# Layer 0's first hidden spectrum taken from modes that are at hand, instead of from a forward transform of q

## The chip, the cores and the metric

The kernel runs on one core of one Trainium2 chip. The metric is the device time of one execution in microseconds (us). Engines: TensorE (PE) multiplies matrices; VectorE (DVE), ScalarE (ACT) and GpSimd (POOL) work elementwise; SyncE (SP) issues the transfers.

## The reference

Two layers follow one another; only the first (L0) is touched. Its input is four batches of T=32 images of 128x128 pixels.

```python
xn = _inorm(xa, norm1_w, norm1_b)          # per image
k, q, v = fno(xn, K..), fno(xn, Q..), fno(xn, V..)   # 32 heads, spectral + skip
p_attn = softmax(scores over the 32 images of a batch)
p = fno(einsum(p_attn, v), Pcw, Psw)
a = _inorm(p + xa, attn_w, attn_b)
an = _inorm(a, norm2_w, norm2_b)
m = gelu(_inorm(spectral(an, m0cw)) + skip(an))
m = _inorm(spectral(m, m1cw)) + skip(m)
x = x + _inorm(m, mon_w, mon_b) + a
```

A spectral convolution keeps 64 x 33 modes of an image's two-dimensional real Fourier transform, multiplies them by a table, and transforms back. p + xa is linear in the modes of x: a mix over the batch's images, and the image's own part.

## The kernel before, in words

A batch of layer 0 has 128 (w) x 32 (images) x 128 (c) values, w on the partitions. The tile framework schedules the work from the program's order and its waits; `behind(a, b)` only keeps a behind b. Buffers belong to tags with a fixed number of them. Instructions of one engine run in order, and DMAs are issued by SP in order. A batch goes through these stages:

1. Front, for the next batch (`image_rows`, `image_moments`, `spectra_of_images`, L388 to L604): ACT squares of x (xx, L395), sums over images by TensorE (rows, L401), the group norm, the modes of x (pz, it, em, std), scaled by n_s (the inverse deviation times norm1_w) into xe, xm, xx, and written to HBM as xd (L559).
2. Attention weights (L653): products pa, pb, scores, softmax; the weights ph leave for HBM and come back as pr. `skip_matrix` (L780) makes bd, the image mix of the skip part: cm on TensorE, cd, cp and bd on DVE.
3. Mix (loop at L961): for five ranges of modes and four quarters of images SP broadcasts xd to xb (four buffers, L969), ACT copies it to PSUM (xw), POOL and DVE multiply by the weights (u, L989, L993), TensorE sums over images (po, L926). Between these, the skip part is turned (pxt) and applied (sk) into q, and the next batch's x is loaded.
4. py (L1027) brings the mixed modes to images, yf (L225, L227 inside `evacuate`, which divides copies over ACT and DVE) is their copy; the inverse (pv L319, four L324) gives p's images, added to q (L1042); bn_stats (L1044) and `stats` give the moments m.
5. `spectra(0, q)`: the forward transform of q (pz L305, px L1123, part, spec), its squares weighed to the variance v0 of the spectral part (L1149 on); the next batch's image rows; `row_products` (y, L342) and `four_images` (L356, L358) give the spectral part's image; the 32 additions of q into x (L1079).
6. GELU: g (L1212), its activation (L1216), bn_stats (L1224), then `spectra(1)` of g, the second variance, and the result added to x.

DVE's bn_stats, additions and copies and ACT's copies share stages 4 to 6. `roots` keeps single instructions for `behind`. Layer 1 lists its work by hand (`tc.manual_schedule`); its first pieces run inside the last batch.

## Time and profile before

| | us |
|---|---|
| runs: median (range) | 2872.17 (2871.64 to 2875.78) |
| profiled execution, of which the span | 2870.23, 2868.6 |
| PE, DVE, ACT, POOL busy in the span | 2720.7, 2175.5, 2315.7, 2035.3 |
| py's start in batches 0 to 3, from the span's start | 131.55, 323.60, 515.70, 707.76 |
| batch 0: m, first g, n_s of the next batch | 160.31, 185.69, 222.06 |
| first d of layer 1 | 833.07 |

Busy times are sums of instructions, which overlap between engines; a long busy time is no bound by itself. A line of the timeline gives start, length, engine, line of the source, operation, output<-inputs, shape and count; in brackets what the engine waited for.

### The profile page before, as it was taken

What the parts mean: (1) busy time and instruction counts of PE and PEld (TensorE: products, weight loads), DVE (VectorE), ACT (ScalarE), POOL (GpSimd) and SP (SyncE); (2) the same over time, 40 slices, a digit from 0 to 9 for tenths busy, and PEclk for the clock granted to TensorE, in tenths of its full rate; (3) what the DMA queues carried; (4) which work ended last, traced back from release to release, by engine and by line L of the source; (5) the groups of instructions that cost most, each with busy time, mean ns of one, the idle gap of its engine ahead of it and who ended that gap; (6) DMA issues with size and microseconds to landing.
All of it is one profiled execution on the core that took longest, in us unless ns stands there. A gap on an engine that the chain in (4) does not pass through costs nothing.

```text
span 2868.6 us, 52910 instructions
## 1 busy us (share of the span) xinstructions
PE 2720.7 (95%) x19638; PEld 1379.6 (48%) x19638; DVE 2175.5 (76%) x4830; ACT 2315.7 (81%) x3243; POOL 2035.3 (71%) x1804
## 2 busy tenths in 40 slices
PE   8898999988879999999999999999999999999996
PEld 5565664654644444445444444544444454444442
DVE  5888788778766677777787776778788677877777
ACT  3555466465459999999999999999999999999990
POOL 2706418137028998998998988898898888878872
PEclk9999999999989999999999999999999999999998
DMA  4403204114030101002101000110100010010000
GB/s 103 125 1 106 88 8 149 39 42 138 3 81 23 41 1 41 8 14 47 40 2 34 16 16 19 41 27 23 41 1 16 20 34 19 16 34 1 16 12 19
DMA packets 151153, 107.72 MB, mean 38 GB/s; under 512 B 36302, under 2 KB 140017, under 8 KB 150897
## 3 DMA queue, kind: packets, MB, share of 16 engines
q1 hardware_dynamic: 147633, 102.26, 13.5%
q8 instruction: 155, 2.54, 0.4%
q10 hardware_dynamic: 3264, 2.10, 0.3%
q14 instruction: 101, 0.83, 0.1%
HBM read 63.86 MB, written 19.50 MB: 29 GB/s over the span
## 4 chain that ended last, share of the span: by engine, by line
PE 60%; ACT 7%; DVE 5%; POOL 3%; issue 2%; DMA 0%; SPq 0%; DVEq 0%; POOLq 0%; ACTq 0%
PE d L1869 26%; PE po L1888 15%; PE px L1770 6%; PE n L1869 5%; ACT r L1938 3%; DVE r L1943 1%; ACT e L1954 1%; DVE xc L1779 1%; ACT r L1950 1%; PE pl L1739 1%; POOL e L1946 1%; PE pz L1571 1%; PE pa L1701 1%; PE pt L1533 1%; PE pz L1586 1%
## 5 line engine op out<-in xcount | busy, mean ns | idle before, releaser
L1943 DVE TENSOR_TENSOR r<-n,r 128x1024 f32<-128x1024 f32 (+1 forms) x1056 | 961.9, 953 | 457.3 <-PE n L1869 327.9
L1938 ACT ACTIVATE r<-d 128x1024 f32<-128x1024 f32 (+1 forms) x1056 | 793.6, 803 | 63.6 <-PE n L1869 51.4
L1946 POOL TENSOR_TENSOR e<-r 128x512 f32<-128x512 f32 x528 | 673.4, 1275 | 213.0 <-DVE r L1943 211.4
L1950 ACT ACTIVATE r<-r 128x1536 f32<-128x1536 f32 x528 | 783.6, 1484 | 16.8
L1947 POOL TENSOR_TENSOR e<-e,r 128x512 f32<-128x512 f32 x528 | 671.8, 1272 | 41.4
L1869 PE MATMUL d<-qe,ke 32*128 32x512 f32 (+3 forms) x2304 | 604.5, 601 | 16.9 <-ACT r L1938 12.8
L1869 PE MATMUL n<-qe,ke 32*128 32x512 f32 (+3 forms) x2304 | 604.6, 601 | 0.0
L1888 PE MATMUL po<-e,kx 128*128 128x512 f32 (+3 forms) x1152 | 594.4, 605 | 3.0 <-POOL e L1959 3.0
L1869 PE MATMUL n<-qf,kf 32*128 32x512 f32 (+3 forms) x2304 | 550.8, 553 | 0.0
L1869 PE MATMUL d<-qf,kf 32*128 32x512 f32 (+3 forms) x2304 | 549.1, 552 | 0.0
L1779 DVE SCALAR_TENSOR_TENSOR xc<-px,wgt,xc 128x128 f32<-128x128 f32 x1024 | 354.5, 349 | 34.9 <-PE px L1770 5.2
L1888 PEld LDWEIGHTS po<-e,kx 128*128 128x128 f32 x1152 | 175.4, 188 | 376.1 <-issue 297.6
L1954 ACT ACTIVATE e<-e 128x512 f32<-128x512 f32 x528 | 324.2, 614 | 14.7 <-POOL e L1947 14.7
L1869 PEld LDWEIGHTS d<-qe,ke 32*128 32x128 f32 x2304 | 176.5, 183 | 302.0 <-ACT r L1938 273.2
L1869 PEld LDWEIGHTS d<-qf,kf 32*128 32x128 f32 x2304 | 219.1, 185 | 164.4 <-issue 152.6
L1770 PE MATMUL px<-we,x2t 128*128 128x512 f32 (+3 forms) x644 | 271.0, 515 | 5.7 <-DVE xc L1779 2.0
L989 POOL TENSOR_TENSOR u<-xb,gb 128x858 f32<-128x858 f32 (+1 forms) x112 | 220.6, 2008 | 42.4 <-PE po L926 37.6
L1869 PEld LDWEIGHTS n<-qf,kf 32*128 32x128 f32 x2304 | 227.5, 185 | 24.8 <-issue 17.2
L1140 POOL TENSOR_TENSOR spec<-part,part 128x512 f32<-128x512 f32 x16 | 25.7, 1609 | 284.8 <-DVE gn_r_t L253 93.0
L993 DVE TENSOR_TENSOR u<-xw,gb 128x858 f32<-128x858 f32 (+1 forms) x208 | 215.6, 1105 | 6.7 <-ACT xw L980 3.1
L1770 PEld LDWEIGHTS px<-we,x2t 128*128 128x128 f32 x644 | 119.3, 193 | 140.4 <-issue 116.8
L1869 PEld LDWEIGHTS n<-qe,ke 32*128 32x128 f32 x2304 | 176.8, 183 | 10.9 <-DVE r L1943 1.5
(425 smaller groups left out, 3409.3 us busy)
## 6 DMA issues: line engine op xcount, KB each, us to landing
xb<-xd SPq DMA_DIRECT2D x128, 214.5 KB
xc<-x SPq DMA_DIRECT2D x29, 512.0 KB
x<-x SPq DMA_DIRECT2D x16, 512.0 KB
qf<-qe SPq DMA_DIRECT2D x64, 128.0 KB
out<-xc SPq DMA_DIRECT2D x15, 512.0 KB
x<-in_x SPq DMA_DIRECT2D x14, 512.0 KB
xb<-xd SPq DMA_DIRECT2D x32, 198.0 KB
kf<-ke SPq DMA_DIRECT2D x32, 128.0 KB
```

The source lines that it names most:

```text
L989: weighed = nc.gpsimd.tensor_tensor(u, xb, gk, ALU.mult)
L993: weighed_last = nc.vector.tensor_tensor(u, xw, gk, ALU.mult)
L1770: nc.tensor.matmul(px[:, at_e : at_e + m], x2t[:, k * P : (k + 1) * P], we[:, own[0] : own[0] + m], start=True, stop=True,)
L1779: nc.vector.scalar_tensor_tensor(xc[:, k], px[:, i], wgt[:, k, e : e + 1], xc[:, k], ALU.mult, ALU.add)
L1869: nc.tensor.matmul(o, k, q, start=turn == 0 or g > 0, stop=turn == 1 or g > 0)
L1888: nc.tensor.matmul(sums[c, h][:, q0 : q0 + c1 - c0], kx[:, jb], e[:, c0:c1], start=jb == 0, stop=is_last and q0 > 2 * P, skip_group_check= ...
L1938: nc.scalar.activation(r[:, g], d, AF.Ln, scale=1.0 / DSCALE)
L1943: nc.vector.tensor_tensor(r[:, g], part, r[:, g], ALU.mult)
L1946: nc.gpsimd.tensor_tensor(e, r[:, 1], r[:, 2], ALU.add)
L1947: nc.gpsimd.tensor_tensor(e, e, r[:, 0], ALU.add)
L1950: nc.scalar.activation(r, r, AF.Exp, scale=-1.0)
L1954: nc.scalar.activation(e, e, AF.Exp)
```

## The change

q's modes are no longer taken from q. They are the mixed modes (py) plus the modes of the batch's images, mixed by the skip matrix. For that xd keeps x's modes times the inverse deviation alone (plain), and norm1_w goes into the value weights (v_raw, hv). Eight DMAs a batch read xd back as xs, which holds images on the partitions. `first_product` adds xs times by_part onto py in PSUM, two DVE products with the first layer's table and a POOL addition make modes_of_q; `to_columns` and `inverse_of` make the image of the spectral part from it. v0 comes from the squares of modes_of_q. The transform of q, its row products and its flat part are gone. `skip_matrix` computes cm by small matmuls and spreads it with one more matmul, and stands behind the second half's row products. Image rows go to four column groups of TensorE instead of two. `unfold`, `edge_row` and the tables carry the scalings along; 133 constant columns and four small table loads are added. Additions into x are divided: 8 ahead of GELU, 8 inside it, 16 behind it.

```diff
...
+    def image_squares(xt, earlier=None):
+        parts = []
         for g in GROUPS:
             xx2 = grp.tile([P, GI, C], F32, name="xx2", tag="pr", bufs=6)
             square = nc.scalar.activation(xx2, xt[:, g : g + GI], AF.Square)
-            if "q_r" in roots:
-                behind(square, roots["q_r"])
+            if earlier is not None:
+                behind(square, earlier)
+            parts.append(xx2)
+        return parts
...
+        rows8 = ps.tile([P, 4, C], F32, name="rows8", tag="b")
+        for g, xx2 in zip(GROUPS, parts):
             for h in range(2):
                 m = g // 4 + h
                 for k, src in enumerate((xt[:, 4 * m : 4 * m + 4], xx2[:, 4 * h : 4 * h + 4])):
+                    r = 64 * k + 32 * (m % 2)
                     mm = nc.tensor.matmul(
-                        rows8[32 * k : 32 * k + 32],
+                        rows8[r : r + 32],
                         one_of_8[:, 7 - m : 39 - m],
                         src,
-                        start=m == 0,
-                        stop=m == 7,
+                        start=m < 2,
+                        stop=m > 5,
                     )
                     products.append(mm)
-        ev = grp.tile([64, 4, C], F32, name="ev", tag="pr", bufs=6)
-        nc.scalar.copy(ev, rows8)
+        ev = grp.tile([P, 4, C], F32, name="ev", tag="pr", bufs=6)
+        copied = nc.scalar.copy(ev, rows8)
+        if earlier is not None:
+            behind(copied, earlier)
...
-                nc.tensor.matmul(s12[k][:, j::4], ev[r, j], ident[r, r], start=True, stop=True)
+                r = slice(64 * k, 64 * k + 64)
+                nc.tensor.matmul(s12[k][:, j::4], ev[r, j], one_row[r], start=True, stop=True)
...
+            plain = grp.tile([P, half, KY], F32, name="plain", tag="fold")
+            nc.vector.tensor_tensor(
+                plain.rearrange("p (k i) y -> p i k y", i=2),
+                std[:, :, :, :KY],
+                yr[:, t].rearrange("p (k i) -> p i k", i=2).unsqueeze(3).to_broadcast([P, 2, pairs, KY]),
+                ALU.mult,
+            )
+            to_rows(xd, t, plain)
...
+            u32 = small.tile([m, T], F32, name="u32", tag="u32")
+            nc.vector.scalar_tensor_tensor(u32, o32, twice_low[:m], yr[:m], ALU.mult, ALU.mult)
...
+            for c0, rev in ((v_raw[:, :, 0, ri], v_rev), (pw[:, :, 0, ri], p_rev)):
+                behind(nc.vector.tensor_tensor(c0, c0, rev[:, :, ri], op), normed[4])
+                nc.vector.tensor_scalar(c0, c0, 0.5, None, ALU.mult)
...
+        root = scalars(ALU.mult, "root", ve, yr)
+        root = scalars(ALU.mult, "roots", same, root)
+        own_root = one("own_root")
+        nc.vector.tensor_reduce(own_root, root, AX.X, ALU.add)
         sel = scalars(ALU.mult, "sel", same, ysc)
+        own = one("own")
+        nc.vector.tensor_reduce(own, sel, AX.X, ALU.add)
+        by_four = small.tile([P, 2, 4, 4], F32, name="by_four", tag="cp")
         for h in range(2):
             r = slice(32 * h, 32 * h + 32)
-            cm = ps.tile([P, T, 16], F32, name="cm", tag="a")
-            mm = nc.tensor.matmul(cm, pv[r].to_broadcast([NH, P]), ph[r], start=True, stop=True)
-            if earlier is not None:
-                behind(mm, earlier)
-            cd = grp.tile([P, T, 16], F32, name="cd", tag="v", bufs=3)
-            nc.vector.tensor_tensor(cd, cm, sel.unsqueeze(2).to_broadcast([P, T, 16]), ALU.mult)
-            nc.vector.tensor_reduce(
-                cp[:, 16 * h : 16 * h + 16], cd.rearrange("p s t -> p t s"), AX.X, ALU.add
+            cm = ps.tile([P, 4], F32, name="cm", tag="a")
+            for t in range(16):
+                j = 32 * (t % 4)
+                mm = nc.tensor.matmul(
+                    cm[j : j + 32, t // 4 : t // 4 + 1], ph[r, :, t], pv[r], start=True, stop=True
+                )
+                if earlier is not None:
+                    behind(mm, earlier)
+            nc.vector.tensor_tensor(
+                by_four[:, h],
+                block.unsqueeze(1).to_broadcast([P, 4, 4]),
+                cm.unsqueeze(2).to_broadcast([P, 4, 4]),
+                ALU.mult,
             )
-        nc.vector.tensor_add(cp, cp, same)
+        cp = ps.tile([P, 2, T], F32, name="cp", tag="a")
+        nc.tensor.matmul(cp[:, 0], alike, by_four.rearrange("p h k j -> p (h k j)"), start=True, stop=True)
+        nc.vector.scalar_tensor_tensor(cp[:, 1], cp[:, 0], own, same, ALU.mult, ALU.add)
         bd = small.tile([P, 4, T], F32, name="bd", tag="bd")
         nc.vector.tensor_tensor(
             bd,
             block.unsqueeze(2).to_broadcast([P, 4, T]),
-            cp.unsqueeze(1).to_broadcast([P, 4, T]),
+            cp[:, 1].unsqueeze(1).to_broadcast([P, 4, T]),
             ALU.mult,
         )
-        return bd
+        by_part = small.tile([P, 2, T], F32, name="by_part", tag="by_part")
+        nc.vector.tensor_tensor(
+            by_part,
+            turn_of.unsqueeze(2).to_broadcast([P, 2, T]),
+            cp[:, 1].unsqueeze(1).to_broadcast([P, 2, T]),
+            ALU.mult,
+        )
+        nc.vector.tensor_scalar(by_part, by_part, own_root, None, ALU.mult)
+        return bd, by_part
...
+    for v in (v_raw.rearrange("p x y r -> p (x y r)"), hv[:, 2:3]):
+        behind(nc.vector.tensor_scalar(v, v, par[:, N1W : N1W + 1], None, ALU.mult), normed[4])
...
+        xy = big.tile([P, 2, KX * KY], F32, name=f"xy_{b}", tag="y")
+        xs = xy[:, 0].rearrange("p (x y) -> p x y", y=KY)
+        yf = xy[:, 1].rearrange("p (t r y) -> p t r y", r=2, y=KY)
+        by_images = [
+            (xs[64 * part + 32 * r : 64 * part + 32 * r + 32, to], front[2][:, r, of])
+            for part in range(2)
+            for r in range(2)
+            for to, of in ((slice(0, KX // 2 + 1), slice(KX // 2, KX + 1)), (slice(KX // 2 + 1, KX), slice(1, KX // 2)))
+        ]
...
+                if x0 and by_images:
+                    to, of = by_images.pop(0)
+                    nc.sync.dma_start(out=to, in_=of)
...
+        modes_of_q = big.tile([P, T, 2, KY], F32, name=f"modes_{b}", tag="spec")
+        pys = {}
+        def rows_of(y0):
             n = min(8, KY - y0)
-            py = ps.tile([P, 8, 2, T], F32, name="py", tag="b")
+            py = ps.tile([P, 8, 2, T], F32, name="py", tag="ba"[y0 // 8 % 2])
+            pys[y0] = py[:, :n]
             for k in range(n):
                 for part in range(2):
                     nc.tensor.matmul(
                         py[64 * part : 64 * part + 64, k],
                         rs[:, :, y0 + k],
                         comb[:, 32 * part : 32 * part + 64],
-                        start=True,
-                        stop=True,
+                        start=k == 0,
+                        stop=k == n - 1,
+                        skip_group_check=True,
                     )
-            evacuate(yf[:, :, :, y0 : y0 + n].rearrange("p t r y -> p y r t"), py[:, :n])
-        if b == 0:
-            mode_tables(weighed_last)
+            copied = nc.scalar.copy(yf[:, :, :, y0 : y0 + n].rearrange("p t r y -> p y r t"), pys[y0])
+            if y0 == GI:
+                roots["rows_copied"] = copied
+        def first_product(y0):
+            py = pys[y0]
+            n = py.shape[1]
+            for k in range(n):
+                for part in range(2):
+                    r = slice(64 * part, 64 * part + 64)
+                    nc.tensor.matmul(
+                        py[r, k], xs[r, :, y0 + k], by_part[r], start=False, stop=k == n - 1, skip_group_check=True
+                    )
+            shape = [P, n, 2, T]
+            table = first_table[:, y0 : y0 + n]
+            one_, two = (
+                grp.tile([P, 8, 2, T], F32, name=f"part{i}", tag="v", bufs=3)[:, :n] for i in (1, 2)
+            )
+            nc.vector.tensor_tensor(one_, py, table[:, :, :1].unsqueeze(3).to_broadcast(shape), ALU.mult)
+            nc.vector.tensor_tensor(
+                two, py[:, :, ::-1], table[:, :, 1:].unsqueeze(3).to_broadcast(shape), ALU.mult
+            )
+            nc.gpsimd.tensor_tensor(
+                modes_of_q[:, :, :, y0 : y0 + n].rearrange("p t r y -> p y r t"), one_, two, ALU.add
+            )
+        starts = range(0, KY, 8)
+        for y0 in starts:
+            rows_of(y0)
+            if y0:
+                first_product(y0 - 8)
+        first_product(starts[-1])
...
+            next_squares = image_squares(loaded, roots["rows_copied"])
+        squares = big.tile([P, T, 2 * KY], F32, name=f"squares_{b}", tag="rs")
+        nc.scalar.activation(squares, modes_of_q.rearrange("p t r y -> p t (r y)"), AF.Square)
+        by_t, y0 = per_image("by_t"), per_image("y0")
+        nc.vector.tensor_reduce(by_t, squares, AX.X, ALU.add)
+        nc.vector.tensor_tensor(y0, squares[:, :, 0], squares[:, :, KY], ALU.add)
+        nc.vector.scalar_tensor_tensor(by_t, y0, half_zero, by_t, ALU.mult, ALU.add)
+        energy_of = sums("ms", ones, by_t, "b")
+        v0 = per_image("v0")
+        nc.vector.tensor_copy(v0, energy_of)
+        qm, qv = stats("q", st, "b")
...
-        spec, sq = spectra(0, q)
-        ahead = []
-        if b + 1 < B:
-            ev, ahead = image_rows(loaded)
-        v0 = weighed("v0", sq, squares, layers[0][2], "a")
-        if ahead:
-            behind(summing["ms"], ahead[-3])
...
+        def to_columns(k):
+            pv2 = ps.tile([2 * KY, 4, P], F32, name="pv2", tag="a")
             for j in range(4):
-                t = image(a, g, j)
+                nc.tensor.matmul(
+                    pv2[:, j],
+                    modes_of_q[:, 4 * k + j].rearrange("p r y -> p (r y)"),
+                    inv,
+                    start=True,
+                    stop=True,
+                )
+            v = grp.tile([2 * KY, 4, P], F32, name="v", tag="v", bufs=3)
+            copied = nc.scalar.copy(v, pv2)
+            if acts:
+                in_order(copied)
+            columns_of_q[k] = v
+        def inverse_of(k):
+            v = columns_of_q[k]
+            if k % 2 == 0:
+                wide[k // 2] = ps.tile([P, 2, 4, C], F32, name="fours", tag="wide")
+            fours[k] = wide[k // 2][:, k % 2]
+            for j in range(4):
+                mm = nc.tensor.matmul(fours[k][:, j], v[:, j], icol, start=True, stop=True)
+            return mm
...
+        def early_rows(k):
+            h, k = divmod(4 * k, GI)
             if k == 0:
                 early.append(grp.tile([P, GI, P], F32, name="z1", tag="z"))
-            in_order(four_rows([gl[:, 8 * h + t] for t in range(GI)], early[h], k, nc.scalar.copy))
-        in_order(four_rows([gl[:, 8 + t] for t in range(GI)], early[1], 4, nc.scalar.copy))
+            in_order(four_rows([gl[:, 8 * h + k + t] for t in range(4)], early[h], k, nc.scalar.copy, 0))
+        early = []
+        columns_of_q = {}
+        for k in range(4):
+            to_columns(k)
+            inverse_of(k)
+        to_columns(4)
+        if b + 1 < B:
+            ev, _ = image_rows(loaded, next_squares)
+            sv = image_moments(ev)
+        to_columns(5)
+        to_columns(6)
+        add_attention(0)
+        gelu(0)
+        gelu(1)
+        inverse_of(4)
+        inverse_of(5)
+        to_columns(7)
+        gelu(2)
+        gelu(3)
+        add_attention(GI, roots["gelu"])
+        inverse_of(6)
+        inverted = inverse_of(7)
+        for k in range(4, 8):
+            gelu(k)
+            early_rows(k - 4)
         if b + 1 < B:
             summed = group_moments(sv, inverted)
-        for g in GROUPS:
-            add_attention(g)
+        for g in GROUPS[2:]:
+            add_attention(g, roots["gelu"])
...
+                if a:
+                    begun = [row_products(spec, a)]
+                    rows_last = roots["rows"]
+                inverted = back(spec, a, last, begun, nc.scalar.copy)
             else:
                 back(spec, a, last_scaled, apart=True)
-            if a == 0 and b + 1 < B:
-                bd = skip_matrix(weights[2], front[4], inverted)
+            if a and b + 1 < B:
+                bd, by_part = skip_matrix(weights[2], front, rows_last)
...
```

## Prediction, made before the changed kernel ran

> **What bounds the kernel now.** I read the slices of the page first, then the waits and timelines of layer 0 by stage. Each digit is a slice of 71.7 us.
>
> ```profile
> span 2868.6 us, 52910 instructions
> ...
> PE   8898999988879999999999999999999999999996
> ...
> DVE  5888788778766677777787776778788677877777
> ```
>
> From slice 13 on (833 us) TensorE never falls below 9: that is layer 1, whose instructions, compared on each engine, have the same order before and after the change. So whatever layer 0 gains or loses reaches the end one for one. Layer 0 is four batches of 192 us (q's first step py starts at 131.55, 323.60, 515.70 and 707.76). Busy times by stage of batch 0 (window; then PE, weight load, VectorE (DVE), ScalarE (ACT), GpSimd (POOL)):
>
> ```profile
> core 0: us, PE busy (x) PEld busy (x) DVE busy (x) ACT busy (x) POOL busy (x), PEclk, DMA share, GB/s
> 131.55:160.31 28.76, 27.43 (x306) 25.79 (x306) 19.24 (x78) 7.69 (x11) 0.00 (x0) 1.00 0.01 2
> 160.31:185.69 25.38, 24.45 (x249) 14.37 (x248) 21.95 (x86) 11.80 (x24) 3.45 (x2) 1.00 0.01 1
> 185.69:203.95 18.26, 14.33 (x129) 8.98 (x128) 16.25 (x71) 16.49 (x41) 0.00 (x0) 1.00 0.01 1
> 203.95:222.06 18.11, 17.75 (x183) 14.73 (x180) 15.95 (x55) 8.73 (x27) 3.02 (x2) 1.00 0.00 1
> 222.06:265.55 43.49, 37.22 (x416) 21.61 (x415) 31.55 (x78) 26.61 (x70) 24.77 (x15) 0.96 0.38 86
> 265.55:323.60 58.05, 52.57 (x641) 25.72 (x640) 54.03 (x53) 35.84 (x82) 51.02 (x26) 1.00 0.56 174
> ```
>
> Rows: (1) py and the inverse of q, up to the moments m; (2) q's forward transform and image rows, up to the first g; (3) GELU; (4) second transform, up to the next batch's n_s; (5) attention; (6) mix. In (2) TensorE is full and DVE fills its waits with additions into x; in (3) and (4) DVE is nearly full: from its timeline, only 1.4 + 1.8 = 3.2 us of waits there; the rest of the unfilled busy sum is issue gaps. So cutting TensorE pays in (2), not in (3) and (4).
>
> **What the Trainium skill says.** "TensorEngine Tiling (Array Packing)", Key Properties: different tiles load weights and multiply in parallel; Instruction Overhead: a matmul costs at least some 60 columns. The trace agrees with the first: the 64x64 products em pass 32 records in 0.82 us (26 ns each), py 132 in 8.03 us (61 ns). "SBUF — State Buffer", Who interferes with whom: a DVE operation with two SBUF inputs is blocked by a GpSimd operation that reads SBUF. The trace agrees: additions into x (two SBUF inputs, 128x128) take 0.35 us, but one took 1.35 at 176.54, inside POOL's spec addition of 175.57 to 177.75, and bd below took 1.97 inside POOL's two u products of 258.78 to 262.77. "DMA: Bandwidth & Descriptors", Issuing engines are not separate DMA queues: all transfers share 16 engines, so new loads meet the mix's broadcasts.
>
> **The change, part by part** (batch 0).
>
> ```profile
> 131.55 8.03 PE L1027 MATMUL py<-cst,rs 128*64 128x64 f32 x132 [0.61 <-ACT rs L1013]
> 140.68 1.96 PE L319 MATMUL pv<-cst,yf 128*66 128x128 f32 x16 [1.09 <-ACT yf L225]
> 142.55 2.05 PE L324 MATMUL four<-icol,v 66*128 66x128 f32 x16
> ```
>
> *First product.* Added: 66 matmuls xs by by_part. At 26 ns 1.7 us, at 61 ns 4.0; they wait between rows of py for ACT's yf copies (1.14 each, all five now on ACT, four squares of 1.05 among them): I add 5.3 (3.4 to 8.0), so the last ends at 131.55 + 8.0 + 5.3 = 144.9. Behind it two DVE products of 0.69 and POOL's strided add, which the trace lacks; the nearest, L1140, takes 1.27 to 2.18. The inverse's v takes its buffer from the y0=24 parts: first v copy at 144.9 + 1.4 + 1.6 = 147.9, first four 148.6 instead of 142.55, 6 us late. The inverse itself stays 13.3 to 14 us (16 groups of about 1 us on PE), m moves from 160.31 to 166.1: **+5.8**.
>
> *q's transform goes.* From m to the first g took 25.4 us. Gone on PE: pz 8.9, px about half of the 13.8 below, y, four, d0, and image rows pass from 0.43 us a pair in two column groups to some 4.1 us in four (po's 0.107 us per record of 429 columns, scaled). v0 now comes from squares of the modes (ACT, 2112 columns, 2.05 by 1.05 per 1024; DVE reduce 2.35), ready while DVE works on the inverse. Left from m to g: the roots' chain of small operations as before, without the waits for ms, and 8 of the 32 additions into x (8 x 0.285 = 2.3), about 10.4 us (9 to 14). New columns and images from the modes (8 groups of 0.97 and 8 of 1.03) run ahead of g on a PE that would idle. g at 176.5 instead of 185.69: **-9.2**.
>
> ```profile
> L1079 DVE SCALAR_TENSOR_TENSOR x<-q,ra,x 128x128 f32<-128x128 f32 x32 | 11.9, 398 | 0.0
> L1123 PE MATMUL px<-z,cst 128*32 128x128 f32 (+1 forms) x192 | 13.8, 314 | 0.0
> L305 PE MATMUL pz<-cst,q 128*128 128x128 f32 x64 | 8.9, 285 | 0.7 <-ACT z L225 0.7
> ```
>
> *Additions into x.* Their 0.0 of idle and their place (165 to 184) show that they filled waits. In the changed order 8 stand inside GELU and 16 behind the last g, ahead of pk: 24 x 0.285 = 6.84 us on a DVE that is full. Also +0.7 for sv, tot and a root; less the 3.2 of waits they can fill, plus 1 for new ones: +5.3. n_s: -9.2 + 5.3 = **-3.9**.
>
> *plain.* Two DVE products a batch (0.72 each, like xx) and u32, less 0.9 of wait at em: pa -3.3. xd's four DMAs per half wait for plain, on SP's queue with the first xb behind them; that has 20 us of cover until the mix.
>
> *Skip matrix.*
>
> ```profile
> 257.28 0.69 DVE L791 TENSOR_TENSOR cd<-cm,sel 128x512 f32<-128x512 f32 x1 [0.43 <-PE cm L787]
> ...
> 260.94 1.97 DVE L797 TENSOR_TENSOR bd<-cst,cp 128x128 f32<-128x128 f32 x1
> ```
>
> DVE loses 2 x (0.69 + 1.02) for about eight small ones (0.2 to 0.4); PE changes four 512-column products for 64 one-column ones (26 to 61 ns, 1.7 to 3.9 us) that now stand behind the last row products, where DVE waits anyway. bd stays exposed to POOL, and by_part has the same shape of operands at half the size. -0.8 (0 to -3; +2 if POOL blocks both).
>
> *New loads.* Eight DMAs a batch, 1.08 MB, through SP among the xb broadcasts; the first waits for the addition into x that frees g (256.47 to 258.8), between the two pr reads, of which the second was issued after that already. In the mix:
>
> ```profile
> GB/s 289 197 167 212 280 250 177 165 196 159 176 156 127 108 184 143 190 197 191 161 23 143 187 171 108 168 154 172 60 153 137 173 173 211 252 274 290 270 267 35
> DMA packets 11736, 10.72 MB, mean 179 GB/s; under 512 B 384, under 2 KB 11727, under 8 KB 11727
> ```
>
> 290 GB/s were reached, 179 used: there is room for a tenth more. DVE (54 of 58) and PE (52.6) bound the mix. +0.5 (0 to +2; 1.08/0.177 = 6.1 if it were full).
>
> Sum per passage to the next batch: -3.3 - 0.8 + 0.5 = **-3.6**, three times: -10.8. **Batch 3** has no next images, no image rows and no next attention; behind its g (764.16, table load 782.6) layer 1's first pieces share DVE and ACT, so part of the 7 us of additions may show again. I count g's -9 to -10 nearly whole: -10 (-6 to -12). **Start:** N1W onto v_raw (0.45) and hv, the pw mirror (4 x 0.12), root, plain 1.3: +3 of DVE, mostly in waits for loads; image rows -0.9; and cd, cp (3.1 us) gone from between batch 0's first u's: together **-1.3** (-4 to +3). Constants grow by 66 KB and four small table loads (the pw mirror among them) join SP's queue: nothing beside the 0.5 MB image loads that gate the start; uncovered, 66 KB at 179 GB/s is 0.4.
>
> Sum: -10.8 - 10 - 1.3 = -22.1, against the profiled execution (2868.6 span + 1.6 around it = 2870.2): 2848. The median of the runs, 2872.2, lies 1.9 above that execution: **2850**.
>
> **Rivals.**
> *DVE is not the bound* behind g: the additions find room (ACT's GELU, 13.3 us of activations and two table loads of 1.28, paces it). Then a passage keeps 8.5: 3 x 8.5 + 10 + 1.3 = 36.8 less, 2835. For: stage (3) has ACT at 16.49, DVE at 16.25. Against: DVE shows almost no waits.
> *The full DVE eats it all:* POOL's adds at 2.2 instead of 1.6, first product at 8 us, and plain uncovered make the passages worth 0 to -1: only batch 3 and the start pay, 2872.2 - 11 = 2861 (2857 to 2870). For: the +6 us ahead of the inverse is a chain across four engines, none of which the trace shows.
> *Slower: loads collide.* The 1.08 MB delays xb and, behind it, the next x, which lands at 321.5 now (last slice above); the new squares need it 5 us into py, and being in ACT's queue between yf copies they would hold py. Cover: 7.5 us from the landing of 129 in batch 0 to 136.5. At 177 GB/s the shift is 6.1, within it; if these 32-partition transfers run at half that rate, xb's late arrival costs the mix up to 12 us a batch, 4 x 12 - 22 = +26: 2898. It decides from (22 + 5.7)/4 = 6.9 us a batch. Against: four xb buffers ahead and 100 GB/s of room.
> The change does do what it says: q's pz, px, y and four are gone from PE's order.
>
> **From cases to numbers.** My forecast 0.55 (own range 2841 to 2858), first rival 0.15, second 0.18 (a third of it within 0.2% of no change), loads 0.12 (a mild form of it also near no change). 0.2%, 5.7 us, is about what these runs can tell. The range from 2834 to 2868 leaves out part of the first rival and the last. Faster 0.82, same 0.08, slower 0.10.
>
> **What would show it.** py plus the first product 13 us long, four at 17 us behind py's start, m at 34.5, g at 45; 16 additions into x directly after the last g's moments; from g to n_s 41 to 42 us instead of 36.4; a period of 188 to 189 us; xb still no releaser of u in the mix; layer 1's first d at about 811. A period at or above 192 refutes the forecast: then look at the POOL add before v, and at DMA as releaser of xw or u.

## The result, and the profile after

The changed kernel takes 2850.57 us (median of 4 runs, 2846.17 to 2854.98) against 2873.08 us before (4 runs): a ratio of 0.9923, 95% interval 0.991 to 0.9935. The prediction was 2850.0. Its profiled execution took 2847.65 us, with a span of 2845.3. The head of its page, with the slices of TensorE and VectorE:

```profile
span 2845.3 us, 53025 instructions
...
PE   8989988989889999999999999999999999999996
...
DVE  5888688678866777767787776768788677877777
```

Each digit is the busy share of one of 40 slices, in tenths. Layer 1 fills TensorE as before. From its first d on, the kernel before took 2035.5 us (2868.6 - 833.07) and the changed one 2034.7 (2845.3 - 810.65): the gain was made in layer 0. Busy times by stage of batch 0, for the same stages and in the same columns as in the table of the prediction (window and length; then PE, weight load, DVE, ACT, POOL, each with its number of instructions; then the granted clock, which is the share of full speed at which TensorE's clock ran, DMA share, GB/s):

```profile
128.09:164.72 36.63, 35.52 (x425) 34.10 (x425) 21.65 (x71) 16.07 (x20) 5.43 (x5) 1.00 0.01 2
164.72:173.89 9.17, 9.17 (x81) 6.21 (x81) 7.17 (x40) 4.29 (x10) 0.00 (x0) 1.00 0.01 2
173.89:198.13 24.24, 20.27 (x193) 17.18 (x193) 22.33 (x96) 19.33 (x44) 0.00 (x0) 0.93 0.00 1
198.13:214.13 16.00, 13.52 (x125) 11.63 (x120) 13.59 (x56) 5.96 (x24) 2.53 (x2) 1.00 0.01 2
214.13:254.93 40.80, 37.10 (x472) 21.74 (x471) 28.54 (x84) 26.09 (x66) 24.79 (x15) 0.96 0.39 85
254.93:313.79 58.86, 52.47 (x641) 25.95 (x640) 53.18 (x55) 36.76 (x82) 51.57 (x26) 1.00 0.66 195
```

The reader is to see three things. The stage up to m (first row) is longer, 36.63 us for 28.76. The stage from m to g (second row) is 9.17 for 25.38. DVE's fill in GELU (third row) is 22.33 of 24.24, and the mix (last row) moves 195 GB/s at a DMA share of 0.66, against 174 at 0.56.

The length of each stage in all batches, in us, from the timelines of both kernels (before / after):

| stage | batch 0 | batch 1 | batch 2 | batch 3 |
|---|---|---|---|---|
| py to the first four | 11.00 / 19.98 | 10.81 / 19.96 | 10.86 / 19.97 | 11.00 / 19.97 |
| four to m | 17.76 / 16.65 | 17.71 / 16.64 | 17.42 / 16.93 | 19.49 / 18.67 |
| m to g | 25.38 / 9.17 | 24.43 / 9.15 | 24.28 / 9.15 | 25.91 / 9.09 |
| g to pk | 18.26 / 24.24 | 18.27 / 25.74 | 18.26 / 25.59 | 21.27 / 22.16 |
| pk to n_s (batch 3: to layer 1's d) | 18.11 / 16.00 | 18.06 / 15.56 | 18.35 / 19.50 | 47.64 / 45.24 |
| n_s to pa | 10.93 / 10.25 | 10.93 / 10.25 | 11.29 / 10.96 | |
| pa to po | 32.56 / 30.55 | 32.55 / 31.02 | 32.58 / 31.82 | |
| po to the next py | 58.44 / 58.86 | 58.48 / 59.27 | 59.49 / 60.22 | |
| sum | 192.44 / 185.70 | 191.24 / 187.59 | 192.53 / 194.14 | 125.31 / 115.13 |

(py starts at 323.99 and 515.23 in the middle batches of the kernel before; the 323.60 and 515.70 given ahead of the prediction are evenly spaced values. Only the end of the mix's window used one of them: 58.05 us there, 58.44 here.)

The span's 23.3 us are therefore: -3.5 up to the first py, -6.7, -3.7 and +1.6 in the three passages, -10.2 in batch 3, and -0.8 in layer 1. This is one execution of each kernel; the four runs of the changed one spread over 8.8 us.

### The profile page after: what moved, and what is told of

It reads as the page before. It is cut to its first block, busy times and chain, and to the rows that moved or that the text cites. A ratio compares the mean times of both kernels' runs of the same rounds, so it can differ in the third digit from the quotient of the medians.

```text
span 2845.3 us, 53025 instructions
## 1 busy us (share of the span) xinstructions
PE 2703.5 (95%) x19678; PEld 1404.2 (49%) x19678; DVE 2140.4 (75%) x4814; ACT 2320.4 (82%) x3223; POOL 2044.0 (72%) x1816
## 3 DMA queue, kind: packets, MB, share of 16 engines
HBM read 68.26 MB, written 19.50 MB: 31 GB/s over the span
## 4 chain that ended last, share of the span: by engine, by line
PE 71%; DVE 9%; ACT 9%; POOL 6%; issue 3%; DMA 2%; SPq 0%; POOLq 0%; DVEq 0%; ACTq 0%
PE d L2031 26%; PE po L2050 16%; PE px L1932 6%; PE n L2031 5%; ACT r L2100 3%; POOL u L1083 2%; PE po L1008 2%; DVE r L2105 1%; ACT e L2116 1%; PE py L1127 1%; DVE xc L1941 1%; PE py L1146 1%; PE pz L309 1%; DMA xb<-xd 1%; ACT r L2112 1%
## 5 line engine op out<-in xcount | busy, mean ns | idle before, releaser
L2112 ACT ACTIVATE r<-r 128x1536 f32<-128x1536 f32 x528 | 783.6, 1484 | 16.7
L1008 PE MATMUL po<-u,pr 128*32 128x429 f32 (+1 forms) x1280 | 149.0, 526 | 25.0 <-POOL u L1083 21.8
```

Of the source, the lines that this page charges most:

```text
L2112: nc.scalar.activation(r, r, AF.Exp, scale=-1.0)
```

## The experiments

All are edits of the changed kernel. Each ratio is to the kernel before; by medians, the changed kernel is at 2850.6, with runs from 2846.2 to 2855.0. Stage lengths are read from the one profiled execution of each version.

### Is DVE the bound behind g? The late additions left out, and moved

```diff
 # no_late_adds
-        for g in GROUPS[2:]:
-            add_attention(g, roots["gelu"])
```

> The changed kernel without the 16 additions of q into x behind the last g, in all four batches (x lacks q in images 16 to 31): the price of their place alone. Theory 1 (they are on the path): 4.6 us a batch in the first three and 2 to 4.6 in the last: 14 to 18 less, 2833 to 2837. Theory 2 (covered): 2848 to 2851.

Measured: 2845.33 (2841.39 to 2850.72), ratio 0.991 (0.9892 to 0.9928). g to pk fell by 3.3, 4.7 and 4.0 us in the first three batches, close to the 4.6 of the additions, so DVE does set that stage. But the whole gained about 5 by medians, not 14 to 18, and the runs of the two versions overlap, so even the 5 is uncertain. Compared with the changed kernel, n_s to pa took 11.27 for 10.25 in batch 0, pa to po 31.81 for 30.55, the mix 60.93 for 58.86; this passage as a whole took 187.54 for 185.70. What came early into attention and mix was lost there. Both theories fail in their sums; the stage's price is confirmed, and how much of it reaches the end is not.

```diff
 # adds_in_attention, first three batches
-        for g in GROUPS[2:]:
-            add_attention(g, roots["gelu"])
...
                 begun.append(row_products(spec, 0, (scores,), range(2)))
+                add_attention(2 * GI, scores)
                 return add_scaled(images_of[2])
...
+                add_attention(3 * GI, softmax)
                 roots["added"] = add_scaled(images_of[3])
```

> The changed kernel, with the 16 additions of q into x that stand behind the last g moved: in the first three batches 8 of them stand on DVE ahead of the row maximum mx and 8 behind less, where DVE waits 2.6 and 1.3 us. Theory 1 (DVE is full from g to n_s and sets the path): g to n_s falls by 16 x 0.285 = 4.6 us a batch, some 1 us of it is given back at the softmax, 3 x 3.5 = 10 us less than the changed kernel: about 2840. Theory 2 (TensorE's chain with its half-clock stretches, or ScalarE, sets n_s and the additions are covered): within 2 us of 2850.6.

Measured: 2852.48 (2849.19 to 2856.66), no gain: the total of theory 2, but not for its reason, since g to pk took 20.08 instead of 24.24 in batch 0. The time came back from pa to po, 36.47 instead of 30.55. The first eight of the moved additions on DVE, and GpSimd at that time (timeline of this version, one line from each engine):

```profile
235.22 5.94 DVE L1218 SCALAR_TENSOR_TENSOR x<-q,ra,x 128x128 f32<-128x128 f32 x8
```

```profile
234.72 4.72 POOL L1494 TENSOR_TENSOR x<-x,g 128x1024 f32<-128x1024 f32 x2
```

Eight additions that cost 0.29 us each elsewhere took 5.94 together. GpSimd's two additions into x ran from 234.72 to 239.44; the first two of DVE's took 2.00 and 2.44 us and ended with them, the other six 0.34 each. The place had a wait on DVE, but GpSimd was reading SBUF in it. That may not be all: in this stage TensorE's granted clock was 0.83 on average, against 0.96 in the changed kernel.

### What does the first product cost? Most of it left out, and its buffers apart

```diff
 # no_first
                 for part in range(2):
                     r = slice(64 * part, 64 * part + 64)
-                    nc.tensor.matmul(py[r, k], xs[r, :, y0 + k], by_part[r], ...)
+                    if k == n - 1:
+                        nc.tensor.matmul(py[r, k], xs[r, :, y0 + k], by_part[r], ...)
```

> The changed kernel with 10 of the 66 matmuls of the first product (the last of each block alone), so that q's modes lack most of the images' own part; DVE's and GpSimd's part of it stays. Theory 1 (their pace of 65 ns a record stands on the path): the first four 4 to 5 us earlier in each batch, where ScalarE's copies and squares then set the pace: 16 to 20 less, 2831 to 2835. Theory 2 (hidden behind ScalarE's yf copies and the squares between them): 0 to 4 less.

Measured: 2832.78 (2827.61 to 2834.99), ratio 0.9863 (0.9848 to 0.9877). Theory 1: py to four takes 14.71, 14.79, 14.79 and 14.76 us instead of 19.97, 5.2 less in each batch. In batch 0 some 3 us of it were lost again before m, where TensorE stood at half clock (granted clock 0.50) from 143.3 to 150.1 us; in batches 1 and 2 m came 5.2 earlier. The timeline of TensorE in the changed kernel, where py's rows, after a wait of 0.61 us for rs, and the first product follow each other without another:

```profile
128.09 4.01 PE L1127 MATMUL py<-cst,rs 128*64 128x64 f32 x64 [0.61 <-ACT rs L1107]
132.03 2.08 PE L1146 MATMUL py<-by_part,xy 64*64 64x64 f32 x32
134.04 2.12 PE L1127 MATMUL py<-cst,rs 128*64 128x64 f32 x32
```

A record of the first product takes 65 ns (2.08/32), one of py 63 to 66; a matmul leaves two records, so the 66 matmuls are 132 records and 8.6 us.

```diff
 # parts_apart
-                grp.tile([P, 8, 2, T], F32, name=f"part{i}", tag="v", bufs=3)[:, :n] for i in (1, 2)
+                grp.tile([P, 8, 2, T], F32, name=f"part{i}", tag="z")[:, :n] for i in (1, 2)
```

> The changed kernel, with the two DVE products of the first product in buffers of another tag (z), so that the inverse's first v copy waits for pv alone and no longer for GpSimd's addition. Theory 1 (the chain DVE, GpSimd, v is on the path): the v copy moves from 147.4 to 145.4, and four, m and g with it: 2 us a batch, 4 x 2 = 8 less, about 2842.6. Theory 2 (the inverse is set by what comes later, by ScalarE's squares or DVE's additions into q): 0 to 2 less.

Measured: 2848.81 (2844.14 to 2851.88), within the scatter of the changed kernel. Theory 2: the first four comes 1.5 us earlier (18.47 for 19.98), and m comes 0.2 earlier, since four to m takes 17.93 for 16.65. DVE's additions into q, their statistics and the sum of the squares (2.35 us) stand there. So the wait of v for GpSimd's addition costs next to nothing.

### The loads: issued twice, and issued last

```diff
 # loads_twice
                     nc.sync.dma_start(out=to, in_=of)
+                    nc.sync.dma_start(out=to, in_=of)
```

> The changed kernel with each of the eight loads of xs issued twice, so 2.16 MB a batch among the xb broadcasts instead of 1.08. Theory 1 (the loads delay xb: in the changed kernel GpSimd waits 1.6 to 3.7 us a mix for it, before the change 0 in the first two and 1.7 in the third): the mix gets 2 to 3 us longer in each batch, 6 to 10 more, 2857 to 2861. Theory 2 (the DMA engines have room, and those waits come from the earlier start of the mix): within 2 us of 2850.6.

Measured: 2875.84 (12 runs, 2870.99 to 2882.35), ratio 1.0016 (1.0007 to 1.0024): 25.3 us more, the whole gain. The mix takes 67.56, 68.70 and 66.51 us instead of 58.86, 59.27 and 60.21. GpSimd's waits in the mix behind batch 0 (us in total, times, longest), in the changed kernel:

```profile
POOL u L1083 <- PE po L1008: 5.3, 4, 3.0
POOL u L1083 <- DMA xb<-xd: 2.4, 3, 1.1
```

With the loads issued twice, and what SyncE waited for there (the same columns; then lines of its timeline):

```profile
POOL u L1084 <- DMA xb<-xd: 9.3, 5, 3.6
SPq L1072 <- DMA xy<-xd: 15.1, 7, 3.0
```

```profile
265.85 0.45 SPq L1071 DMA_DIRECT2D xy<-xd  x1
269.24 0.31 SPq L1072 DMA_DIRECT2D xy<-xd  x1
```

Before the change GpSimd waited there for po alone:

```profile
POOL u L989 <- PE po L926: 8.6, 7, 3.9
```

The first load of a pair goes out at 265.85, and the second, into the same buffer, only at 269.24: SyncE waits until the first has landed, and the xb broadcasts behind it in SyncE's order wait with it. That is 15.1, 16.5 and 14.9 us in the three mixes; the changed kernel has no such wait. Meanwhile the mix moved 187 GB/s, less than the changed kernel's 195, at a DMA share of 0.67. So xb was late, as theory 1 has it, but the run cannot price 1.08 MB more of transfers: some or all of its time is an issuing engine that stands still. Whether the DMA engines had room for more stays open.

```diff
 # loads_last
-                if x0 and by_images:
-                    to, of = by_images.pop(0)
-                    nc.sync.dma_start(out=to, in_=of)
...
+        for to, of in by_images:
+            images_read = nc.sync.dma_start(out=to, in_=of)
+            behind(images_read, broadcast)
         if b + 1 < B:
-            loaded = load(b + 1, broadcast)
+            loaded = load(b + 1, images_read)
...
-            if y0 == GI:
+            if y0 == 4 * GI:
                 roots["rows_copied"] = copied
```

> The changed kernel with the eight loads of xs issued behind the last xb broadcast instead of among them, the next batch's x behind them, and the next images' squares on ScalarE behind all five yf copies. Theory 1 (the mix stands at the limit of the DMA engines, so the loads cost time there: doubled they cost 25 us): the mix goes back to 58.0 to 58.5 us from 58.9, 59.3 and 60.2, xb is no releaser of u in it: 3 to 5 us less, 2846 to 2848. Theory 2 (the mix waits for xb because it starts earlier, whatever else is loaded): mix as in the changed kernel, 2850 to 2852; or the late loads hold the first product, four later than 20 us behind py.

Measured: 2850.06 (5 runs, 2848.11 to 2853.66), no difference. The mix is 58.16, 58.14 and 60.45 us, and no wait of GpSimd ends on xb in the first two; in the third some still do, 2.8 us in all. So the loads' place among the broadcasts cost 0.7 and 1.1 us in two mixes and nothing in the third. It is given back by py to four, 20.71 to 20.81 for 19.97: the mix of theory 1, the total of theory 2. Whether the loads delay xb by the bytes they move or by standing ahead of it in SyncE's order is not separated.

```diff
 # loads_last_parts: loads_last, and as in parts_apart
-    ... name=f"part{i}", tag="v", bufs=3)
+    ... name=f"part{i}", tag="z")
```

> The same with the first product's DVE results in buffers of tag z. Theory 1: as when it was done alone, four 1.5 us earlier and m only 0.2 us, since DVE's additions into q and their statistics set the inverse: 0 to 2 us less than with the loads last alone. Theory 2 (with the squares gone from between the yf copies the v copies come earlier still): 4 us less than with the loads last alone.

Measured: 2854.33 (2853.24 to 2856.72), 4 us more than with the loads last alone, which neither theory had. four comes 1.1 to 1.2 us earlier in the first three batches and four to m takes 18.94 to 19.22 for 16.64: m comes 1.1 to 1.4 later there, and 1.0 earlier in batch 3. DVE's sum of the squares now stands behind one of q's additions instead of two and waits 0.89 us for ScalarE; whether that is the cause was not tried.

### The skip matrix at its new place in its old form

```diff
 # skip_as_before
...
+            cm = ps.tile([P, T, 16], F32, name="cm", tag="a")
+            mm = nc.tensor.matmul(cm, pv[r].to_broadcast([NH, P]), ph[r], start=True, stop=True)
...
+            nc.vector.tensor_tensor(cd, cm, sel.unsqueeze(2).to_broadcast([P, T, 16]), ALU.mult)
+            nc.vector.tensor_reduce(cp[:, 16 * h : 16 * h + 16], cd.rearrange("p s t -> p t s"), AX.X, ALU.add)
...
+        nc.vector.tensor_add(cp, cp, same)
```

> The changed kernel with the image mix of the skip matrix computed as before the change (four matmuls of 512 columns, cd and cp on DVE), at its new place. Theory 1 (the small form pays by itself): DVE's 2 x (0.69 + 1.02) come back between the additions into x and the first u, 1 to 2 us a passage and 2 to 3 in front of the first mix: 5 to 9 more, 2856 to 2860. Theory 2 (the gain of that stage came from its new place behind the row products): within 2 us of 2850.6.

Measured: 2857.98 (2856.28 to 2863.35), 7.4 more: theory 1. The first py comes at 131.93 instead of 128.09, so the small form is the gain at the start; how much of that goes through TensorE's clock is not separated (half clock from 71.5 to 78.3 us in the kernel before, from 73.3 to 76.7 in this version, nowhere in that mix in the changed one). In the later passages cd and cp stand between the first u's, and the mix takes 62.96, 61.71 and 67.31 us in the profiled execution, the slowest of the four. pa to po keeps its gain with the old form (30.33, 29.46 and 30.84): that gain is not the small form's.

### The clock of TensorE in GELU

Batches 1 and 2 gained less than batch 0. Two windows of batch 1, and two of batch 2, changed kernel (the columns as above; the granted clock is the third figure from the end):

```profile
364.00:372.00 8.00, 8.00 (x46) 8.00 (x46) 5.78 (x25) 4.30 (x12) 0.00 (x0) 0.60 0.01 3
372.00:386.00 14.00, 10.30 (x102) 7.60 (x101) 13.84 (x62) 11.03 (x25) 0.00 (x0) 1.00 0.00 0
```

```profile
573.02:582.00 8.98, 6.91 (x46) 4.67 (x46) 6.20 (x34) 1.12 (x4) 1.26 (x1) 0.62 0.00 0
582.00:592.52 10.52, 9.47 (x89) 8.56 (x87) 8.58 (x25) 4.68 (x20) 1.27 (x1) 1.00 0.01 2
```

The trace also records each change of the granted clock. It is 0.50 from 179.2 to 182.6 us in batch 0, from 363.5 to 370.3 in batch 1, from 551.3 to 558.1 and from 575.1 to 582.0 in batch 2. Before the change these stages of the first three batches had 1.00 throughout. In all fourteen kept traces such stretches last 3.41 us or a multiple of it, and within one trace they all start whole multiples of 3.41 us apart.

What they cost can be read across versions. Eight of them, the changed kernel among them, have DVE's late additions in their place and nearly the same work from g to pk; in three batches each that is 24 stages:

| half clock within the stage | stages | g to pk, us |
|---|---|---|
| 3.41 us | 8 | 23.4 to 24.7 |
| 6.83 us | 14 | 24.8 to 25.7 |
| 10.24 us | 2 | 26.8 |

So about 1 us goes with each 3.41 us at half clock. From pk to n_s of batch 2 the same eight take 17.96 and 17.98 us with one such stretch, 19.1 to 19.5 with two. No run set the clock, so this is a relation, not an experiment.

```diff
 # moments_dense
-                nc.tensor.matmul(s12[k][:, j::4], ev[r, j], one_row[r], start=True, stop=True)
+                nc.tensor.matmul(s12[k][:, :, j::4], ev[r, j], one_row[r].unsqueeze(1).to_broadcast([64, 8, 8]), ...)
...
```

> The changed kernel with the 16 small matmuls of the image moments widened from 8 to 64 columns (eight equal copies of which one is read). Theory 1 (TensorE's clock falls to 0.5 in the GELU stage because these small matmuls leave it nearly unused for some microseconds): the stretches at 179 to 183, 363 to 371 and 551 to 559 us are gone, and the second and third batch go from g to pk in 24.2 us instead of 25.7: some 3 us less, 2847. Theory 2 (its waits set the clock, not these matmuls): the stretches stay, time as the changed kernel.

Measured: 2851.12 (2846.79 to 2856.18). The stretches did not go: 178.6 to 182.0 in batch 0, 366.4 to 369.8 and 376.6 to 383.4 in batch 1, 564.3 to 567.7 and 578.0 to 584.8 in batch 2. Theory 1 is refuted. Stretches and total are what theory 2 forecast; its reason, TensorE's waits, is not shown. That they moved says little of the small matmuls, for they move as much between versions that leave GELU alone: in batch 1 the stretch begins 4.0 us behind g in the changed kernel and 12.9 behind it with the loads issued twice.

### GpSimd takes the additions

```diff
 # adds_on_pool
-        for g in GROUPS[2:]:
-            add_attention(g, roots["gelu"])
+        for g in GROUPS[2:]:
+            prod = grp.tile([P, GI, C], F32, name="prod", tag="pr", bufs=6)
+            nc.gpsimd.tensor_tensor(
+                prod, q[:, g : g + GI], ra[:, g : g + GI].unsqueeze(2).to_broadcast([P, GI, C]), ALU.mult
+            )
+            nc.gpsimd.tensor_tensor(xr[:, g : g + GI], xr[:, g : g + GI], prod, ALU.add)
```

> The changed kernel with the 16 additions of q into x behind the last g done by GpSimd, as four operations of 1024 elements (a product and an addition for each group of 8 images), while GpSimd is idle in GELU. Theory 1 (they cost 4 us of DVE there, of which attention and mix give part back, as when they were left out: 2845.3): 2843 to 2847. Theory 2 (GpSimd's reads of SBUF block DVE's operations with two SBUF inputs, and the moments wait for it): no better than 2850.

Measured: 2882.51 (2877.97 to 2883.78), ratio 1.0038 (1.0024 to 1.0051): 32 more than the changed kernel. GpSimd began as soon as ra was known, and m to g took 16.91 us for 9.17. Three of DVE's small operations in that chain, 128x32 elements that cost 0.18 to 0.19 elsewhere:

```profile
171.34 1.90 DVE L270 TENSOR_TENSOR r_t<-r_t,r_ve 128x32 f32<-128x32 f32 x1
...
173.43 2.32 DVE L271 TENSOR_SCALAR r_t<-r_t 128x32 f32<-128x32 f32 x1
...
175.93 2.32 DVE L272 TENSOR_TENSOR r<-r,r_t 128x32 f32<-128x32 f32 x1
```

and GpSimd at that time:

```profile
171.06 2.14 POOL L1413 TENSOR_TENSOR prod<-q,ra 128x1024 f32<-128x1024 f32 x1 [1.39 <-PE rows L429]
173.16 5.04 POOL L1416 TENSOR_TENSOR x<-x,prod 128x1024 f32<-128x1024 f32 x2
```

Each DVE operation ends within 0.05 us of a GpSimd operation (173.24 and 173.20, 175.75 and 175.71, 178.25 and 178.20). The Trainium skill ("SBUF — State Buffer", Who interferes with whom) says that the port pair is locked for a whole instruction, also against tensor_scalar in the modes that use both ports; the trace agrees that whole operations are waited for, and the mode of this tensor_scalar is not shown in it. g to pk did not fall either (24.68, 24.93 and 23.47): TensorE stood at half clock for 11 to 17 us of it. How much of the 32 us is the port and how much the clock is not separated.

```diff
 # loads_last_pool: loads_last, and inside the loop over the last four groups of g
+            for g in GROUPS[2:] if k == 4 else ():
+                (product as above)
+                behind(product, roots["gelu"])
+                (addition as above)
```

> The loads last, and the 16 additions of q into x behind the last g done by GpSimd as four operations of 1024 elements that start behind the activations of the fifth group of g. Theory 1 (GpSimd hurts only DVE operations that read two operands from SBUF; g reads one from PSUM): g to pk 20 to 21 us instead of 24 to 26, some of it given back in attention, 4 to 8 us less than with the loads last alone, 2839 to 2843. Theory 2 (it blocks the moments, g's statistics or the sums behind pk as it blocked DVE for 1.9 to 2.3 us at a time ahead of g): no gain or a loss of up to 8.

Measured: 2880.14 (2877.63 to 2887.05). m to g is 16.94. `behind` sets an order without a wait: GpSimd began its first product at 168.73, 0.4 us behind ra, long before the activations it was put behind. So this version repeated the one before and says nothing of its theories.

```diff
 # pool_in_gelu
         add_attention(0)
+        ra_late = small.tile([P, T], F32, name="ra_late", tag="va")
+        nc.vector.scalar_tensor_tensor(ra_late, hq, 0.0, ra, ALU.mult, ALU.add)
+        for g in GROUPS[1:]:
+            (product with ra_late and addition on GpSimd, as above)
         gelu(0)
...
-        add_attention(GI, roots["gelu"])
...
-        for g in GROUPS[2:]:
-            add_attention(g, roots["gelu"])
```

> The changed kernel with the 24 additions of q into x that stand in and behind GELU done by GpSimd as six operations of 1024 elements. In the two GpSimd versions before, they began as soon as ra was known, ahead of g, and blocked DVE's chain there; here they read a copy of ra that DVE makes from hq, at the end of that chain, so they can begin with g only, when DVE's operations read at most one operand from SBUF. Theory 1 (it is the second SBUF operand that is blocked, and DVE's work behind g is on the path): m to g 9.2 to 9.6 us as in the changed kernel, g to pk 18.5 to 20 instead of 24 to 26, of which attention gives 2 to 3 back as it did when additions were left out: 2838 to 2846. Theory 2 (GpSimd reading SBUF blocks g and its statistics too): g to pk 25 us or more, 2850 or above.

Measured: 2836.31 (2835.69 to 2837.93), ratio 0.9881 (0.9865 to 0.9898): 14 us less than the changed kernel by medians, 12 by the ratios, and the fastest version that computes everything. Theory 1: m to g stays at 9.20 to 9.41, g to pk is 20.68, 18.95, 20.35 and 19.89, a little over its range. GpSimd and DVE at the start of GELU:

```profile
174.36 3.75 POOL L1400 TENSOR_TENSOR prod<-q,ra_late 128x1024 f32<-128x1024 f32 x2 [26.05 <-DVE ra_late L1397]
178.07 4.66 POOL L1403 TENSOR_TENSOR x<-x,prod 128x1024 f32<-128x1024 f32 x2
```

```profile
178.82 0.48 DVE L1375 BATCH_NORM_STATS2 st<-g 128x6 f32<-128x128 f32 x2
179.22 0.33 DVE L1363 SCALAR_TENSOR_TENSOR g<-q,hq,fours 128x128 f32<-128x128 f32 x1
```

g, with one operand in SBUF and one in PSUM, and its statistics keep their 0.33 and 0.24 us inside GpSimd's addition. Attention again gives part back (n_s to pa 11.0 to 11.3, pa to po 31.8), so batch 0 gains nothing by it, batches 1 and 2 gain 4.0 and 5.9. Of the 5.9, 2.3 lie between pk and n_s, where this version has no half-clock stretch.

## Why the prediction was right, point by point

The total held: 2850.0 against 2850.57. It was a sum in which several terms were off and cancelled, so its closeness is in part luck.

- **First product and m: the mechanism was right, the term too small.** I added 5.3 us to py (3.4 to 8.0) and put m 5.8 later. From py to pv it is 16.7 us, 7.6 more than the 9.1 before; four came 19.98 behind py where I had 17, and m 7.9 later after py. The mis-sized term is the 66 matmuls "at 26 ns 1.7 us, at 61 ns 4.0": a matmul leaves two records, and the rate of em, which used four tiles of the array, was not to be had by matmuls that use two. Measured, 65 ns a record, 8.6 us.
- **GpSimd's addition before v** was feared in both directions (1.3 to 2.2 us). It took 1.28, and its wait is covered by DVE's work on q, as the separate buffers showed.
- **From m to g** I had 10.4 us and got 9.17; g, put at 45 us behind py, is at 45.8. With m 2.1 late and the chain 1.2 short, these two errors partly cancelled. The squares, put at 2.05 us where 1.05 per 1024 columns makes 2.17, took 1.96.
- **From g to n_s** I had 41.7 and got 40.2, 41.3 and 45.1. That DVE sets g to pk was right: 16 additions left out took 3.3 to 4.7 us off. Against py, n_s came 4.5 us earlier in batch 0, where I had 3.9, but only 2.2 in batch 1, and 2.0 later in batch 2. What I had put at nothing is TensorE's clock: batch 1 has 6.83 us at half clock between g and n_s and batch 2 has 13.65, against 3.41 in batch 0 and none before the change.
- **plain** I charged with +0.6 net at pa; n_s to pa became shorter, 0.7, 0.7 and 0.3 us: it is hidden, and something I had not listed went with it, which was not traced further.
- **Skip matrix:** -0.8 in the passages; pa to po gave -2.0, -1.5 and -0.8, and gives them in the old form too. At the start I had -1.3 in all, and it was -3.5. The small products of cm took 0.98 us there, not 1.7 to 3.9. The first po began 0.9 earlier (69.86 for 70.72) and the 2.4 us wait behind it went with cd and cp. The run with the old form put the first py 3.8 us later.
- **Loads:** +0.5 a mix was right (0.4, 0.8, 0.7). xb became a releaser of u, 1.6 to 3.7 us a mix, which I had said it would not; most of that stands in the place of waits for po (5.3 us in the first mix instead of 8.6). "There is room for a tenth more" held for that tenth; no run shows whether there is more.
- **Batch 3:** -10, measured -10.2, of which -7.8 up to pk. The other 2.4, from pk to layer 1's d (45.24 us), is the shortest of the same eight versions (45.2 to 48.2), so this agreement is in part the luck of one execution.
- **Sum of the passages:** -10.8, measured -8.8, spread over -6.7, -3.7 and +1.6 where I had three equal ones. The third passage, 194.1 us, is over the 192 that I had named as refuting the forecast; the mean, 189.1, is close to the 188 to 189 that I expected.

Of the rivals, the slower one had the right place: the loads do delay xb. Its price did not come: 0.4 to 0.8 us a mix against the 6.9 us a batch from which it decides. The 6.3 us a batch of the loads issued twice look like its 6.1 for a full DMA, but SyncE's waits of some 15 us a mix stand in them. That DVE is no bound behind g is refuted for its stage, and the full 8.5 us a passage did not arrive. That DVE eats everything was nearest in batch 2. There additions and clock are not separated: without the late additions that passage is 4.2 us shorter, and its stretch behind pk is gone too.

## What to carry to other kernels

Price a stage by what its neighbours leave of a gain. Leaving additions out took 12.6 us off the four GELU stages and gave the whole about 5, within the scatter of the runs; moving more of them to GpSimd took 17.9 off and gave 14. Measure the end as well as the stage.

An experiment that issues a transfer twice into one buffer makes the second wait for the first. Look at the waits of the issuing engine before the extra time is called bandwidth.

Work moved to GpSimd was free here beside g (one operand in SBUF, one in PSUM) and beside bn_stats, and cost much beside small operations with all operands in SBUF, one of them a tensor_scalar. Only a data dependence, not an order, kept it in its place.

## What the runs showed of the hardware beyond the expected

- 64x64 matmuls that fill two of four tiles pass at 65 ns a record (64 columns), those that fill four at 26 (72 columns). An estimate from these: 130 and 104 ns for each tile, so the number of tiles would explain most of the difference.
- TensorE's clock stood at 0.50 for 3.41, 6.83 or 10.24 us at a time in GELU, on a grid of 3.41 us in every trace. The Trainium skill ("TensorE: Matmul & The Clock Gate", Part 1) says that an idle window of some 3.4 us of a free-running count halves the clock. The lengths and the grid fit such windows, but TensorE's records show it busy but for 0.8 us between m and the stretch of batch 1; why its use counted as idle stays open.
- DVE operations of 0.18 us took 1.90 and 2.32 beside GpSimd operations on SBUF, among them one with a single tensor operand.
